# Graph attention, layer 2: the weighted sums of two beats issued as a pair, ahead of a later beat's scores

## Chip, cores and metric

One core of a Trainium2 chip runs the whole kernel. The metric is device time in microseconds (us). Before the change it is 3083.47 us, the median of three runs (3078.59 to 3084.39). The execution that the profile shows took 3076.43 us, and its instructions span 3074.7 us.

## What is computed

Eight graphs of 2048 nodes with 128 features pass through four attention layers that share one adjacency matrix. Each layer normalises x, applies a ReLU, and adds its attention to x. Layers 0, 1 and 3 are additive graph attention. Layer 2, which the change concerns, is dot-product attention with four heads of 32 features and no weights:

```
x = input_tensor.reshape(B, S, H, F // H)
scores = jnp.einsum('bihk,bjhk->bhij', x, x)
scores = leaky_relu(scores); masked where adj == 0
probs = jax.nn.softmax(scores, axis=-1)
out = jnp.einsum('bhij,bjhk->bihk', probs, x)
```

## The kernel before

**Two kinds of work are interleaved by hand.** Layers 0, 1 and 3 are cut into *tokens*. A token is one block of 128 source nodes against one half of the target nodes. Its `front` (line 396) is one VectorE operation that builds a 128x1024 tile `zg`. Its `back` (line 406) is eight matmuls of 129 columns, which add into PSUM banks 1 to 3. There are three `zg` buffers.

Layer 2 is cut into *beats*: 64 to an image (four heads by 16 source blocks), 512 in all. Beat q has three steps:

- `scores` (line 497): four TensorE matmuls of 512 columns into two pairs of PSUM banks, each pair followed by one ScalarE exponential (line 500) that writes half of a 128x2048 tile `z`. There are three `z` buffers. The bank pairs 4-5 and 6-7 are used in turn, and other steps (transposes, projections) use them too.
- `mask` (line 506): one VectorE operation that multiplies `z` by the adjacency and sums it.
- `weigh` (line 514): the sums. Four TensorE matmuls, each with 32 columns of weights at its own quarter of the array (`tile_position=(0, c * HD)`) and 512 columns of `z`, add into PSUM bank 0. When `weigh` is done, that `z` buffer is free for the scores of beat q + 3.

**The driving loop** (lines 626 to 641 before) walks over the beats. In pass q it issues the scores of q + 2, the mask of q + 1, one token if it is due, the sums of q, and further tokens until as many have been issued as the image's span asks for. The planner fixes only how tokens are spread over beats: images 1 to 5 have about 96 real tokens to 64 beats, image 0 about 34, image 6 63 and image 7 18, counted between the first sums of one image and of the next. The small stages of neighbouring layers (statistics, normalising, transposes, projections) hang on particular tokens.

**The order on an engine is not the order of the text.** The framework that builds the program schedules instructions by its own estimate of when they can start, and fixes the order on each engine. So four matmuls of a `weigh` may stand together, or as one and three with other matmuls between them. An engine then works through its own list in that order and waits where an operand is missing.

Of the kernel before, what the change touches and what calls it, by code (L numbers as in the profile page):

```python
# [37 lines left out]
def adj_preln_d4(ctx: ExitStack, tc: tile.TileContext, x, adj, w0, a0, w1, a1, w3, a3,  # L38
# [186 lines left out]
    def fast(ctx):  # L225
# [26 lines left out]
        def passed(us):  # L252
            for w in list(waiting):
                w[0] -= us
                if w[0] <= 0:
                    waiting.remove(w)
                    w[1]()
# [342 lines left out]
        def token():  # L600
            t = tokens[done[0]]
            if t:
                fronts(done[1] + 2)
                t[0].back(t[1])
                done[1] += 1
            for piece in pieces.get(done[0], ()):
                piece[0](*piece[1:])
            done[0] += 1
            passed(TOKEN_US)

        def beat(what, q):
            if q < B * 64:
                getattr(heads[q // 64], what)(q % 64)
# [12 lines left out]
        for q in range(B * 64):  # L626
            k, s = divmod(q, 64)
            t0, t1 = spans[k]
            until = t0 + (t1 - t0) * (s + 1) / 64
            beat("scores", q + 2)  # L630
            beat("mask", q + 1)
            if done[0] < until - 0.5:
                token()
            beat("weigh", q)
            passed(BEAT_US)
            if q % NB == 3 and q // NB + 1 < B * HEADS:
                g = q // NB + 1
                heads[g // HEADS].load(g % HEADS)
            while done[0] < until - 0.5:
                token()  # L640
# [173 lines left out]
    with tc.If(ok > 0) as arm:  # L814
        with ExitStack() as inner:
            fast(inner)
# [27 lines left out]
```

## Time and profile before

| What | Value |
|---|---|
| Time, median of 3 | 3083.47 us |
| TensorE (PE) busy | 2874.4 us, 93% |
| VectorE (DVE) busy | 2549.0 us, 83% |
| ScalarE (ACT) busy | 1808.8 us, 59% |
| Layer 2's beats run | from 383.7 us (first scores) to 2942 us (last sums) |
| Mean granted TensorE clock | 0.973 |
| DMA | 137.90 MB, mean 45 GB/s |

The span has three parts: the adjacency and the first tokens alone (to 384 us), the beats with tokens among them (to 2942 us), and the last tokens alone. The matmuls are float32. Each of those on lines 406 and 514 stands in the profile as two records, so "x8" on line 514 is one whole `weigh`, and "x16" on line 406 is one token. The ends of matmul records are modelled; what one costs is better read from the start of one group to the start of the next.

### The profile page before, as it was taken

To read this page: it belongs to the slowest core of one execution; us is meant where nothing else is said; L and a number is where in the kernel's file an instruction comes from. 1 tells how busy PE (TensorE), PEld (TensorE's weight loads), DVE (VectorE), ACT (ScalarE), POOL (GpSimd) and SP (SyncE) were. 2 spreads that over 40 slices of the span, in tenths; PEclk is the share of its full clock that TensorE was granted. 3 is DMA by queue.
4 is the path that set the end of the run, shared out by engine and by line. 5 is a ranking of instruction groups with operands and counts; after the bars stand their busy time and mean duration, and the time that the engine had idled before them with its cause. 6 is when DMAs were issued, how large, how long until landed. Compare 5 with 4: busy or idle time off the path is not lost.

```text
span 3074.7 us, 50065 instructions
## 1 busy us (share of the span) xinstructions
PE 2874.4 (93%) x20412; PEld 2112.7 (69%) x20415; DVE 2549.0 (83%) x3765; ACT 1808.8 (59%) x3113; POOL 168.2 (5%) x54
## 2 busy tenths in 40 slices
PE   3699989999999999999999999999999999988977
PEld 2699936677776776777677776777767766633657
DVE  5477769888898988988798997989879889987867
ACT  2343276758566558655676556665576666678652
POOL 1000000000010010000100001000000000000000
PEclk8699999999999999999999999999999999999998
DMA  6200411211113102121111212111021111312000
GB/s 223 55 1 1 97 41 45 56 32 32 32 35 69 49 17 67 32 59 25 49 44 27 52 32 66 32 39 45 15 73 32 42 28 39 79 38 55 8 8 22
DMA packets 141999, 137.90 MB, mean 45 GB/s; under 512 B 81728, under 2 KB 115136, under 8 KB 135616
## 3 DMA queue, kind: packets, MB, share of 16 engines
q1 hardware_dynamic: 134656, 125.87, 16.4%
q0 software_dynamic: 1152, 8.39, 0.7%
q8 instruction: 162, 2.65, 0.4%
q10 hardware_dynamic: 5952, 0.35, 0.2%
q14 instruction: 77, 0.63, 0.1%
HBM read 101.01 MB, written 33.55 MB: 44 GB/s over the span
## 4 chain that ended last, share of the span: by engine, by line
PE 72%; DVE 11%; ACT 8%; POOL 4%; issue 3%; DMA 2%; ACTq 0%; SPq 0%; POOLq 0%; DVEq 0%
PE ps L406 37%; PE ps L514 15%; PE ps L497 14%; DVE z L506 4%; DVE zg L396 4%; ACT z L500 3%; POOL rstdx L189 3%; PE ps L335 3%; ACT h L298 2%; PE ps L308 2%; PE ps L390 1%; DMA raw<-in_adj_dram 1%; DVE st L195 1%; POOL rstdh L189 1%; ACT wh L374 1%
## 5 line engine op out<-in xcount | busy, mean ns | idle before, releaser
L406 PEld LDWEIGHTS ps<-y,zg 128*128 128x128 f32 x12288 | 1499.2, 193 | 277.6 <-issue 132.5
L406 PE MATMUL ps<-y,zg 128*128 128x129 f32 x12288 | 1559.8, 279 | 18.3 <-DVE zg L396 14.8
L500 ACT ACTIVATE z<-ps,shift 128x1024 f32<-128x1024 f32 x1024 | 1098.7, 1117 | 679.7 <-PE ps L497 640.2
L506 DVE SCALAR_TENSOR_TENSOR z<-z,edge 128x2048 f32<-128x2048 f32 x512 | 1168.2, 2285 | 153.1 <-ACT z L500 151.2
L396 DVE SCALAR_TENSOR_TENSOR zg<-r,cr,edge 128x1024 f32<-128x1024 f32 x768 | 973.6, 1278 | 153.9 <-PE ps L406 125.6
L497 PE MATMUL ps<-m,s 128*128 128x512 f32 x2048 | 702.3, 438 | 59.9 <-ACT z L500 32.6
L514 PE MATMUL ps<-z,v 128*32 128x512 f32 x4096 | 645.9, 607 | 12.2 <-DVE z L506 12.2
L497 PEld LDWEIGHTS ps<-m,s 128*128 128x128 f32 x2048 | 339.1, 191 | 385.0 <-ACT z L500 152.3
L298 ACT ACTIVATE h<-x,nmrx,rstdx 128x128 f32<-128x128 f32 x512 | 216.2, 490 | 143.0 <-DVE nmrx L191 127.4
L189 POOL TENSOR_TENSOR rstdx<-varx,neg_half 128x16 f32<-128x16 f32 x32 | 123.4, 3859 | 2348.3 <-DVE varx L187 2069.9
L514 PEld LDWEIGHTS ps<-z,v 128*32 128x32 f32 x4096 | 93.5, 108 | 135.4 <-issue 63.4
L195 DVE BATCH_NORM_STATS2 st<-x 128x6 f32<-128x128 f32 x512 | 126.4, 268 | 7.9 <-DMA x<-in_x_dram 7.9
L335 PE MATMUL ps<-rhs,h_t 128*128 128x130 f32 x768 | 111.9, 290 | 3.2 <-ACT z L500 2.3
L335 PEld LDWEIGHTS ps<-rhs,h_t 128*128 128x128 f32 x768 | 100.1, 201 | 15.8 <-ACT z L500 11.8
L308 PE MATMUL ps<-ident,h 128*128 128x128 f32 x512 | 85.8, 284 | 24.1 <-ACT h L298 17.5
L325 ACT COPY h_t<-ps 128x512 f32<-128x512 f32 x96 | 56.1, 584 | 83.2 <-PE ps L308 83.0
L308 PEld LDWEIGHTS ps<-ident,h 128*128 128x128 f32 x512 | 61.5, 145 | 45.7 <-issue 19.3
L196 DVE BATCH_NORM_AGGREGATE mv<-st 128x2 f32<-128x6 f32 x512 | 82.1, 168 | 0.2
L191 DVE SCALAR_TENSOR_TENSOR nmrx<-mv,rstdx 128x16 f32<-128x16 f32 x32 | 5.6, 176 | 90.2 <-POOL rstdx L189 90.2
L429 ACT ACTIVATE oe<-ps,rs 128x128 f32<-128x128 f32 x128 | 53.5, 418 | 43.8 <-DVE rs L422 43.8
L351 ACT ACTIVATE y<-ps,y 128x128 f32<-128x128 f32 x256 | 73.2, 370 | 0.0
L391 ACT COPY r<-ps 128x1024 f32<-128x1024 f32 x48 | 48.4, 1011 | 41.0 <-PE ps L390 40.8
(95 smaller groups left out, 1061.9 us busy)
## 6 DMA issues: line engine op xcount, KB each, us to landing
s<-halves SPq DMA_DIRECT2D x256, 128.0 KB, 2.7
m<-halves SPq DMA_DIRECT2D x64, 512.0 KB, 5.5
raw<-in_adj_dram SPq DMA_DIRECT2D x8, 1024.0 KB, 7.3
raw<-in_adj_dram POOLq DMA_DIRECT2D x8, 1024.0 KB, 9.3
values<-h SPq DMA_DIRECT2D x32, 256.0 KB, 2.3
halves<-hi SPq DMA_DIRECT2D x128, 64.0 KB, 1.7
halves<-lo SPq DMA_DIRECT2D x128, 64.0 KB, 1.7
v<-values SPq DMA_DIRECT2D x32, 256.0 KB, 3.4
```

The lines of the kernel that those rows point to most:

```text
L189: nc.gpsimd.tensor_tensor(out=rstd, in0=var, in1=neg_half, op=OP.pow)
L195: nc.vector.bn_stats(out=st[:, n, :], in_=rows)
L196: nc.vector.bn_aggr(out=mv[:, n, :], in_=st[:, n, :])
L298: nc.scalar.activation(h, self.x[:, n, :], AF.Relu, scale=self.rstd[:, n:n + 1], bias=self.nmr[:, n:n + 1])
L308: nc.tensor.transpose(pk[:, k, :], self.h[q][:, k, :], ident)
L335: nc.tensor.matmul(pv[:, k, :C + 2], lhsT=self.h_t[q][:, k * P:(k + 1) * P], rhs=rhs, start=True, stop=True)
L396: nc.vector.scalar_tensor_tensor(z, self.r[half], self.cr[:, 0, jb:jb + 1], edge[:, jb, half * HN:(half + 1) * HN], op0=OP.max, op1=OP.mult)
L406: nc.tensor.matmul(ps[:, self.sums[half][i // 3], k * CE:(k + 1) * CE], lhsT=z[:, i * P:(i + 1) * P], rhs=self.y[:, jb, :], start=(jb == 0 ...
L497: nc.tensor.matmul(ps[:, lo + c, :], lhsT=self.S[h, jb // HB][:, at:at + P], rhs=self.M[h][:, (c2 * 2 + c) * 512:(c2 * 2 + c + 1) * 512], ...
L500: nc.scalar.activation(z[:, c2 * HN:(c2 + 1) * HN], ps[:, lo:lo + 2, :].rearrange("p b t -> p (b t)"), AF.Exp, bias=shift)
L506: nc.vector.scalar_tensor_tensor(self.z[s], self.z[s], 1.0, edge[:, jb, :], op0=OP.mult, op1=OP.mult, accum_out=self.den[:, h, jb:jb + 1])
L514: nc.tensor.matmul(ps[c * HD:(c + 1) * HD, 0, :], lhsT=self.V[h][:, jb, :], rhs=z[:, c * 512:(c + 1) * 512], start=jb == 0, stop=jb == NB - 1,
```

## The change

The sums leave the end of the pass. In each odd pass, the sums of the even beat before it and of its own beat are issued one after the other, at the head of the pass, in front of the scores of q + 2. In even passes none are issued. The purpose is to let the eight column-quarter matmuls of two beats stand next to each other on TensorE. The number and shape of the instructions stay the same, and so do the buffers.

```diff
             until = t0 + (t1 - t0) * (s + 1) / 64
+
+            if q % 2:
+                beat("weigh", q - 1)
+                beat("weigh", q)
             beat("scores", q + 2)
             beat("mask", q + 1)
             if done[0] < until - 0.5:
                 token()
-            beat("weigh", q)
             passed(BEAT_US)
```

## The prediction

> **What bounds the kernel now.** I read the busy shares first, then the chain that ended last, the groups of instructions, the stages, and last the timeline of TensorE alone.
>
> ```profile
> PE 2874.4 (93%) x20412; PEld 2112.7 (69%) x20415; DVE 2549.0 (83%) x3765; ACT 1808.8 (59%) x3113; POOL 168.2 (5%) x54
> PE 72%; DVE 11%; ACT 8%; POOL 4%; issue 3%; DMA 2%; ACTq 0%; SPq 0%; POOLq 0%; DVEq 0%
> PE ps L406 37%; PE ps L514 15%; PE ps L497 14%; DVE z L506 4%; DVE zg L396 4%; ACT z L500 3%; POOL rstdx L189 3%; PE ps L335 3%; ACT h L298 2%; PE ps L308 2%; PE ps L390 1%; DMA raw<-in_adj_dram 1%; DVE st L195 1%; POOL rstdh L189 1%; ACT wh L374 1%
> ```
>
> TensorE is busy 93% of the span and carries 72% of the chain; the sums (L514) alone are 15% of it. The groups give the prices:
>
> ```profile
> L406 PE MATMUL ps<-y,zg 128*128 128x129 f32 x12288 | 1559.8, 279 | 18.3 <-DVE zg L396 14.8
> L500 ACT ACTIVATE z<-ps,shift 128x1024 f32<-128x1024 f32 x1024 | 1098.7, 1117 | 679.7 <-PE ps L497 640.2
> L506 DVE SCALAR_TENSOR_TENSOR z<-z,edge 128x2048 f32<-128x2048 f32 x512 | 1168.2, 2285 | 153.1 <-ACT z L500 151.2
> L396 DVE SCALAR_TENSOR_TENSOR zg<-r,cr,edge 128x1024 f32<-128x1024 f32 x768 | 973.6, 1278 | 153.9 <-PE ps L406 125.6
> L497 PE MATMUL ps<-m,s 128*128 128x512 f32 x2048 | 702.3, 438 | 59.9 <-ACT z L500 32.6
> L514 PE MATMUL ps<-z,v 128*32 128x512 f32 x4096 | 645.9, 607 | 12.2 <-DVE z L506 12.2
> ```
>
> The idle columns matter. ACT waits for PE (640.2 us), DVE for PE and ACT, while PE's sums wait for the mask only 12.2 us in all, and its scores for the exponential (to free a bank pair) 32.6 us. PE sets the pace. The stages (span, then PE, PEld, DVE, ACT busy) show where that is less true; they are image 0, image 3 and image 7 of layer 2:
>
> ```profile
> 384.00:644.00 260.00, 249.74 (x1482) 140.69 (x1484) 208.75 (x233) 186.54 (x277) 5.76 (x2) 0.99 0.20 49
> 1355.00:1714.00 359.00, 348.96 (x2533) 259.84 (x2536) 312.56 (x464) 222.67 (x386) 19.98 (x5) 1.00 0.17 42
> 2719.00:2943.00 224.00, 200.96 (x1124) 99.72 (x1116) 185.30 (x239) 166.38 (x219) 9.65 (x2) 0.97 0.12 28
> ```
>
> In image 3 PE lacks 10 of 359 us, and DVE still has 46 us to spare. In image 7, with few tokens, PE lacks 23 of 224. Now PE's timeline (start, duration, group):
>
> ```profile
> 1016.08 1.05 PE L514 MATMUL ps<-z,v 128*32 128x512 f32 x2
> 1017.06 2.05 PE L406 MATMUL ps<-y,zg 128*128 128x129 f32 x16
> 1019.04 1.06 PE L514 MATMUL ps<-z,v 128*32 128x512 f32 x6
> 1020.03 1.20 PE L497 MATMUL ps<-m,s 128*128 128x512 f32 x4
> 1021.07 1.95 PE L406 MATMUL ps<-y,zg 128*128 128x129 f32 x16
> 1022.94 1.07 PE L514 MATMUL ps<-z,v 128*32 128x512 f32 x8
> ```
>
> One `weigh` is split here: a quarter alone takes 1017.06 - 1016.08 = 0.98 us, the other three 0.99 us. A whole one (x8) takes the same, 0.996 us in the median of 326 of them, start to start. So time is paid by the run, not by the matmul. And another place shows what a second set costs in the same run:
>
> ```profile
> 751.06 1.90 PE L514 MATMUL ps<-z,v 128*32 128x512 f32 x10
> 752.89 1.19 PE L497 MATMUL ps<-m,s 128*128 128x512 f32 x4
> ```
>
> Ten records are a whole set and one quarter more: 1.83 us, so the second set added 1.83 - 0.98 = 0.85 us.
>
> **What the Trainium skill says.** "TensorEngine Tiling (Array Packing)", Tiling Modes, says that a change of tiling mode (not merely of tile) drains the engine. The trace agrees with a cost at the borders: within a run, token records start 0.112 us apart, so 16 should take 1.79 us; the token between two sums above takes 1019.04 - 1017.06 = 1.98 us, 0.19 us more for one way out and one way in. "TensorE: Matmul & The Clock Gate", Part 3, says that column tiles run at once, some 4 ns apart; here the quarters start 7 ns apart. The same page, Part 2, says that matmuls stay in program order and only weight loads are pulled ahead, so a waiting sum holds everything queued behind it on PE.
>
> **The change, part by part.** Nothing is added or removed in kind: 2048 matmuls on L514, 2048 on L497 and 6144 on L406 in both. What differs is the built order on each engine, which I counted.
>
> *Sums on PE.* Before, the 2048 matmuls stand in 600 runs: 410 of four, and 84 of one and 86 of three from split beats. Counting one set for each time a quarter of the array comes round again, they make 607 sets. After, there are 457 runs, 113 of them of eight, and 579 sets. A run costs 0.98 + 0.19 = 1.17 us, a further set in it 0.86 us (two passes of 0.43 us, the middle of the readings). Before: 600 x 1.17 + 7 x 0.86 = 708 us. After: 457 x 1.17 + 122 x 0.86 = 640 us. The saving is 68 us. By image, from the same count and prices: 14 in image 0, 9 in each of images 1 to 4, 11 in image 5, 7 in image 6, and only 2 in image 7, where the order hardly changes. All lies on the engine that sets the end.
>
> *Scores on PE.* 795 runs become 750. A split costs nothing: one to four matmuls take 0.32, 0.57, 0.79 and 1.03 us, 0.24 each and about 0.08 a run, and the token before starts them 0.08 us early (0.030 instead of 0.112 us after its last record). Zero. The other matmuls, ACT, DVE and DMA keep their counts and durations: zero, under PE's work.
>
> *The wait for the mask.* A pair now needs the mask of its second beat. Behind a waiting sum on PE stand the scores of q + 2 and the tokens; ACT waits for those scores, and DVE for ACT. From the last score matmul to a ready `z` at least 1.12 (exponential) + 2.29 + 0.08 (mask and its read-out) + about 0.1 = 3.6 us pass, and up to 1.28 more if a token's `zg` is ahead on DVE: 4.9 us. I summed the PE work, at the prices above, between each beat's last score and its first sum in the built order. In images 1 to 6 the mean is 8.9 to 11.5 us before and 8.6 to 10.6 after: two beats of slack, hence no wait. Under 5 us are 43 beats before and 56 after, nearly all in images 0 and 7. There PE idles 10.3 + 22.9 = 33 us before, with 42 such beats: 0.79 us each. Thirteen more: +10 us. The bounds are 0 (idle in those images has other causes too) and 13 x 2.4 = 31 us (a whole mask each).
>
> *The wait for a bank pair.* Without sums between them, the scores of two beats come closer: after a pair, "scores, one token, scores" is 1.9 us apart, then a long stretch follows. A pair of banks is free 1.12 us plus a hop after its matmuls, if ACT isn't in other work (each normalising row holds it 0.49 us). Reuse within 2.5 us of PE work happens 210 times before and 311 after. The 32.6 us of before are 0.155 us each: 101 x 0.155 = +15 us (bounds 0 and 30).
>
> *Tokens in twos.* The after order has 86 runs of exactly two tokens, before 20, with the same three `zg` buffers. All gaps before L406 in the beats' part are 13 us before; I allow +8 (bounds 0 and 20). In image 3 DVE goes from 312.6 / 359 = 87% to 312.6 / 350 = 89%, so it doesn't become the bound.
>
> Sum: -68 + 10 + 15 + 8 = -35 us, 3083.5 - 35 = 3048 us.
>
> **Rivals.** *A, the forecast*, 3048 us. *B, the waits eat the gain*: uneven spacing makes ACT and DVE work in bursts and PE idle for them. With every wait at its upper bound, 31 + 30 + 20 = 81 us, nothing is left; at about four fifths, 65 us, it ends at 3080. For it: DVE is at 87% and ACT sits in the loop PE, ACT, DVE, PE of image 7. Against: the mean slack of 8.6 us and more. *C, slower*: pairing makes PE stand at every run of eight until the second mask is done. If 113 runs wait 0.75 us (somewhat over half a `zg`), 85 us are added: 3083.5 - 68 + 85 = 3100. For it: the text puts the mask of q only one pass ahead of its sum, where it used to be more. Against: the built order, which keeps two beats between scores and sums. *D, the whole gain* with no more than a few us of new waits: 3020 us; for it, the 12.2 us of mask waits in the whole span.
>
> **How the numbers follow.** A 0.55, B 0.25, C 0.13, D 0.07. A and D are faster by over 0.2% (6.2 us); of B I give 0.10 to faster, 0.08 to no difference and 0.07 to slower; C is slower. Faster 0.72, same 0.08, slower 0.20. The range runs from 3022, which takes in half of D, to 3090, which takes in B and leaves out C. What is left out is about 0.04 + 0.13, with a little of A's and B's edges.
>
> **What would show it.** L514 should have about 457 runs, with x16 groups whose starts lie 1.83 us from the next group's; the total of those runs start to start falls by some 40 us, and the rest shows in tokens of 1.81 to 1.88 us where they were 1.98. DVE's and ACT's busy times stay at 2549 and 1809. The idle before L514 for the mask should stay under some 25 us, that before L497 for the exponential under some 50. Image 3 should take about 353 us, image 0 about 250, image 7 224 to 230. It is wrong if a second set in a run costs 0.98 us after all (then 122 x 0.12 = 15 us less), if sums wait for the mask in the images with many tokens, or if the idle before L497 doubles.

## The result and the profile after

The changed kernel takes 3039.82 us (median; 3036.10 to 3041.98), the kernel before, timed beside it on the same chip, 3083.93 us. The ratio is 0.9857, with a 95% interval of 0.9839 to 0.9876: 44 us less (38 to 50). The prediction was 3048 us.

The profiled spans are 3036.1 and 3074.7 us, a difference of 38.6 us. It lies in the beats (2559.2 to 2526.4 us, -32.8) and ahead of them (383.7 to 376.2 us, -7.5, in code that the change doesn't touch). The tail after the beats takes 133.5 us where it took 131.8. The other 5 us of the 44 aren't in the profiles: the execution profiled of the kernel before was 7 us under its median, that of the changed one 2 us under. The images in us, from first sums to first sums (image 0 from its first scores, image 7 to the last sums):

| Image | 0 | 1 | 2 | 3 | 4 | 5 | 6 | 7 |
|---|---|---|---|---|---|---|---|---|
| before | 260 | 352 | 359 | 359 | 362 | 362 | 281 | 224 |
| after | 251 | 347 | 356 | 356 | 357 | 354 | 279 | 226 |

First the busy shares and the chain that ended last, of the kernel after:

```profile
PE 2816.8 (93%) x20415; PEld 2116.3 (70%) x20415; DVE 2544.2 (84%) x3765; ACT 1804.7 (59%) x3113; POOL 165.3 (5%) x54
PE 67%; DVE 15%; ACT 9%; POOL 4%; issue 3%; DMA 1%; ACTq 0%; POOLq 0%; SPq 0%; DVEq 0%
```

TensorE's share of the chain fell from 72% to 67%, VectorE's rose from 11% to 15%. DVE's and ACT's busy times didn't move. So more of the end now hangs on other engines, although TensorE has less to do. The groups say where (line, engine, operation, then busy us and mean ns, then the idle time before it and what ended it):

```profile
L406 PE MATMUL ps<-y,zg 128*128 128x129 f32 x12288 | 1526.9, 278 | 22.0 <-DVE zg L396 16.1
L500 ACT ACTIVATE z<-ps,shift 128x1024 f32<-128x1024 f32 x1024 | 1093.5, 1117 | 683.7 <-PE ps L497 636.0
L506 DVE SCALAR_TENSOR_TENSOR z<-z,edge 128x2048 f32<-128x2048 f32 x512 | 1166.6, 2282 | 147.6 <-ACT z L500 146.2
L497 PE MATMUL ps<-m,s 128*128 128x512 f32 x2048 | 689.5, 435 | 58.1 <-ACT z L500 26.6
L514 PE MATMUL ps<-z,v 128*32 128x512 f32 x4096 | 600.8, 607 | 28.3 <-DVE z L506 27.9
```

The sums lost 45 us of modelled busy time. Their wait for the mask went from 12.2 to 27.9 us. The scores' wait for the exponential fell, from 32.6 to 26.6 us. The stages of images 0, 3 and 7 (span, then PE, PEld, DVE, ACT busy):

```profile
376.00:627.00 251.00, 239.37 (x1497) 142.64 (x1496) 209.22 (x235) 184.10 (x276) 5.76 (x2) 0.98 0.23 52
1331.00:1686.00 355.00, 341.83 (x2526) 260.95 (x2519) 311.19 (x464) 222.53 (x385) 19.98 (x5) 1.00 0.17 42
2677.00:2903.00 226.00, 200.06 (x1123) 100.53 (x1121) 186.19 (x240) 166.71 (x219) 9.66 (x2) 0.96 0.13 27
```

In image 3 PE now lacks 13 of 355 us, where it lacked 10 of 359. And TensorE's timeline, in image 3, shows the pairs themselves (start, duration, group):

```profile
1598.73 3.74 PE L406 MATMUL ps<-y,zg 128*128 128x129 f32 x32
1602.39 1.92 PE L514 MATMUL ps<-z,v 128*32 128x512 f32 x16
1604.25 1.20 PE L497 MATMUL ps<-m,s 128*128 128x512 f32 x4
1605.28 1.95 PE L406 MATMUL ps<-y,zg 128*128 128x129 f32 x16
1606.98 1.17 PE L497 MATMUL ps<-m,s 128*128 128x512 f32 x4
```

A pair takes 1604.25 - 1602.39 = 1.86 us from its start to the next group's. The token after the scores takes 1606.98 - 1605.28 = 1.70 us, since it has no sum on either side. Over the whole trace a run of 8 records takes 996 ns in the median, one of 16 takes 1854 ns (113 of them). A token takes 1.98 us between two sums, 1.81 after sums and before scores, 1.88 the other way round, 1.70 between two scores. Added up start to start, the sums fell from 639.4 us in 600 runs to 597.8 us in 457, by 41.6 us.

The beats' time on TensorE can be cut into work (start to next start, less the idle that the trace shows) and that idle:

| us in the beats | before | after | difference |
|---|---|---|---|
| sums, without idle | 606.4 | 570.7 | -35.7 |
| tokens, without idle | 1103.2 | 1086.4 | -16.8 |
| scores, without idle | 594.9 | 588.2 | -6.7 |
| other matmuls, without idle | 169.5 | 174.7 | +5.2 |
| idle that the trace shows | 85.2 | 106.4 | +21.2 |

The work fell by 54 us, and 21 us came back as idle: for the mask +15.7, for the exponential -6.2 ahead of scores and +3 ahead of other matmuls, for ScalarE's small steps (rows and copies, lines 298, 301, 325, 346, 391, 430 and 432) about +10, for `zg` 0 (7.5 us in both).

One thing doesn't show as idle: TensorE's granted clock. The trace has it over time, and in the beats it is either 1.0 or 0.5. One place where it is 0.5, in the changed kernel (a stretch as above, with the clock after the busy times, then TensorE's timeline):

```profile
1129.00:1135.70 6.70, 5.39 (x24) 5.29 (x25) 3.73 (x5) 4.35 (x9) 0.00 (x0) 0.50 0.37 98
1130.31 0.80 PE L497 MATMUL ps<-m,s 128*128 128x512 f32 x1 [2.85 <-DVE lo L470]
1130.90 6.94 PE L406 MATMUL ps<-y,zg 128*128 128x129 f32 x40
```

The 40 records of tokens take 6.87 us to the next group (at 1137.77 us), where 40 x 0.112 = 4.48 us would do. Over the whole of the beats, records of tokens start 112 ns apart (median) at a clock of 1.0 and 214 ns at 0.5. So such a stretch costs about half of the time in it in which TensorE works. Before, 58 us of the beats are at 0.5 (49 of them work), after, 65 us (50 work): by this estimate 24 and 25 us are lost, which doesn't change the account. Between experiments the loss differs more, and is given below where it matters. In the changed kernel each of the eleven such stretches has 1.3 us or more of TensorE's idle time in the 7 us before it; that waits bring the clock down is likely, but no run varied one of the two alone.

### The profile page after: what moved, and what is told of

Read it like the earlier page. It is cut to its first block, busy times and chain, and to the rows that moved or that the text cites. A ratio compares the mean times of both kernels' runs of the same rounds, so it can differ in the third digit from the quotient of the medians.

```text
span 3036.1 us, 50090 instructions
## 1 busy us (share of the span) xinstructions
PE 2816.8 (93%) x20415; PEld 2116.3 (70%) x20415; DVE 2544.2 (84%) x3765; ACT 1804.7 (59%) x3113; POOL 165.3 (5%) x54
## 4 chain that ended last, share of the span: by engine, by line
PE 67%; DVE 15%; ACT 9%; POOL 4%; issue 3%; DMA 1%; ACTq 0%; POOLq 0%; SPq 0%; DVEq 0%
PE ps L406 34%; PE ps L514 14%; PE ps L497 13%; DVE z L506 6%; DVE zg L396 5%; POOL rstdx L189 3%; ACT z L500 3%; PE ps L335 3%; ACT h L298 2%; PE ps L390 1%; PE ps L308 1%; DVE st L195 1%; POOL rstdh L189 1%; DMA raw<-in_adj_dram 1%; ACT wh L374 1%
## 5 line engine op out<-in xcount | busy, mean ns | idle before, releaser
L406 PE MATMUL ps<-y,zg 128*128 128x129 f32 x12288 | 1526.9, 278 | 22.0 <-DVE zg L396 16.1
L497 PE MATMUL ps<-m,s 128*128 128x512 f32 x2048 | 689.5, 435 | 58.1 <-ACT z L500 26.6
L514 PE MATMUL ps<-z,v 128*32 128x512 f32 x4096 | 600.8, 607 | 28.3 <-DVE z L506 27.9
L298 ACT ACTIVATE h<-x,nmrx,rstdx 128x128 f32<-128x128 f32 x512 | 216.8, 490 | 128.9 <-DVE nmrx L191 123.3
L189 POOL TENSOR_TENSOR rstdx<-varx,neg_half 128x16 f32<-128x16 f32 x32 | 121.6, 3801 | 2317.8 <-DVE varx L187 2097.1
L514 PEld LDWEIGHTS ps<-z,v 128*32 128x32 f32 x4096 | 102.0, 108 | 200.1 <-issue 101.1
L308 PEld LDWEIGHTS ps<-ident,h 128*128 128x128 f32 x512 | 60.9, 144 | 52.5 <-issue 20.9
L325 ACT COPY h_t<-ps 128x512 f32<-128x512 f32 x96 | 56.1, 584 | 59.2 <-PE ps L308 59.2
L390 PE MATMUL ps<-ident,cr 128*128 128x128 f32 x384 | 53.9, 287 | 16.0 <-ACT r L391 11.0
```

Source lines behind the costliest of these rows:

```text
L189: nc.gpsimd.tensor_tensor(out=rstd, in0=var, in1=neg_half, op=OP.pow)
L298: nc.scalar.activation(h, self.x[:, n, :], AF.Relu, scale=self.rstd[:, n:n + 1], bias=self.nmr[:, n:n + 1])
L308: nc.tensor.transpose(pk[:, k, :], self.h[q][:, k, :], ident)
L390: nc.tensor.transpose(pk[:, k, :], self.cr[:, 1, n:n + 1].to_broadcast([P, P]), ident)
L406: nc.tensor.matmul(ps[:, self.sums[half][i // 3], k * CE:(k + 1) * CE], lhsT=z[:, i * P:(i + 1) * P], rhs=self.y[:, jb, :], start=(jb == 0 ...
L497: nc.tensor.matmul(ps[:, lo + c, :], lhsT=self.S[h, jb // HB][:, at:at + P], rhs=self.M[h][:, (c2 * 2 + c) * 512:(c2 * 2 + c + 1) * 512], ...
```

## The experiments

Two theories stood at the start. The first: TensorE pays by the run and by the set, so a kernel with fewer runs and sets is faster by that much, less small waits. The second: it is the place of the sums or their pairing as such that counts, or TensorE isn't the bound and the saved work turns into waits. The ratios are to the kernel before, beside which each was timed; runs and sets are counted in the built order, as in the prediction.

### The pair at the end of the pass, and single sums at its head

The change has two parts: sums in pairs, and sums in front of the scores. The pairing alone (e1):

```diff
             if done[0] < until - 0.5:
                 token()
-            beat("weigh", q)
+            if q % 2:
+                beat("weigh", q - 1)
+                beat("weigh", q)
             passed(BEAT_US)
```

> The sums of two beats are issued as a pair, but where they stood before: at the end of the odd pass, behind the scores and a token. Theory 1 (TensorE pays 1.17 us for each run of sums and 0.86 us for each further set in it): the built order has 485 runs and 664 sets, against 600 and 607 before and 457 and 579 after, so the sums cost 721 us against 708 and 640; the time is 3085 to 3105 us, no gain. Theory 2 (pairing as such pays): 113 or so pairs are kept, 3040 to 3055 us.

Measured: 3119.77 us, ratio 1.0125 (1.0107 to 1.0144), slower than either end of what the first theory gave. Pairs there are: 115 runs of eight, as many as in the changed kernel (113). But 235 runs are of one or three matmuls, where 170 were before, so there are 485 runs and 664 sets, more than the 607 of before, and the sums take 704.5 us start to start. That pairs as such pay, the second theory of this run, is thereby out. One row of the groups of this kernel tells what else happened:

```profile
L500 ACT ACTIVATE z<-ps,shift 128x1024 f32<-128x1024 f32 x1024 | 1092.1, 1117 | 805.2 <-PE ps L514 584.5 <-PE ps L497 218.7
```

The exponential now mostly waits for the sums (584.5 us; 35.9 before). With three `z` buffers, the scores of q + 2 can't be exponentiated until the sums of q - 1 are done, and these come last in the pass. So an order in the text that pairs the sums is not enough: behind the scores, it ties the `z` buffers up. (By the counts, 13 of the 41 us above the kernel before are dearer sums. Visible idle in the beats is 104 us instead of 85, and the clock estimate gives a loss of 34 us instead of 24. That the buffers bring this idle is argued from the row, not tested.)

The place alone (e2):

```diff
+            beat("weigh", q)
             beat("scores", q + 2)
             beat("mask", q + 1)
             if done[0] < until - 0.5:
                 token()
-            beat("weigh", q)
```

> The sums of each beat stand at the head of their own pass, in front of the scores, not paired. Theory 1: 575 runs and 576 sets, 674 us, 34 us less work than before; but 82 beats instead of 43 have under 5 us of TensorE work between their last score and their sums, at up to 0.79 us each, so 10 to 34 us is given back: 3050 to 3085 us. Theory 2 (the place ahead of the scores is what pays): 3040 us as in the changed kernel.

Measured: 3074.13 us, ratio 0.9989 (0.9979 to 0.9999). There are 575 runs and 576 sets. By the prediction's prices that is 575 x 1.17 + 0.86 = 674 us, 34 less than before; 3 to 5 us came. The work on TensorE in the beats did fall by 34 us, but 30 us came back as idle: the sums' wait for the mask rose to 24.5 us and the scores' wait for the exponential to 41.8. The place alone gives next to nothing, and the pairs where the sums stood before lose: neither half of the change has its gain.

### Whole sums without pairs

The kernel before, with the four matmuls of a `weigh` kept together by a higher priority in the scheduler (e3):

```diff
                 for c in range(4):
-                    nc.tensor.matmul(ps[c * HD:(c + 1) * HD, 0, :], lhsT=self.V[h][:, jb, :],
+                  with tc.high_priority():
+                    nc.tensor.matmul(ps[c * HD:(c + 1) * HD, 0, :], lhsT=self.V[h][:, jb, :],
```

> The kernel before, with the sums' instructions at the highest priority in the scheduler, so that no set is split: 507 runs, 512 sets, no pairs to speak of. Theory 1: the sums cost 598 us, 110 us less than before and 42 us less than after, and the groups on line 514 sum to about 500 us start to start. But they come soon after their masks: 194 beats have under 5 us of slack instead of 43. If each costs 0.79 us, 119 us come back and the time is about 3090 us; if only the real excess counts, 3000 to 3050 us. The idle before the sums for the mask must be well over 28 us. Theory 2 (splits cost little, waits decide): slower than before, over 3100 us.

Measured: 3045.33 us, ratio 0.9888 (0.9872 to 0.9905), with 507 runs and 512 sets; the sums take 535.1 us. So hardly any pair is needed for three quarters of the change's gain: whole sums do it. Priced, it should have given 507 x 1.17 + 5 x 0.86 - 708 = -110 us; a third came. The sums' row in the groups shows one taker of the rest:

```profile
L515 PE MATMUL ps<-z,v 128*32 128x512 f32 x4096 | 555.4, 615 | 51.3 <-DVE z L506 50.4
```

The visible idle of TensorE in the beats is 132 us here, 47 more than before. And its clock is at 0.5 in 99 us of the beats, where it was in 58: by the estimate above a loss of 41 us instead of 24.

### All sums in pairs

The sums of an even beat are made to depend on the mask of the odd one, so that the scheduler can't separate them, with a priority that keeps all eight matmuls together (e4):

```diff
+                  with tc.high_priority(offset=100):
+                    mm = nc.tensor.matmul(ps[c * HD:(c + 1) * HD, 0, :], lhsT=self.V[h][:, jb, :],
...
+                    if s % 2 == 0:
+                        tc.add_manual_dep(mm.ins, self.mk[s + 1].ins.name, mybir.DependencyInfo(
+                            mybir.DependencyClass.Sync, mybir.DependencyReason.DATA), reason="pair")
```

> The changed kernel, with the first sums of a pair made to wait for the mask of its second beat, and the sums ahead of other work in the scheduler: all 512 sets stand in 256 runs of eight. Theory 1: the sums cost 520 us, 188 us less than before and 120 less than after; the slack is as before (45 beats under 5 us), bank pairs are reused within 2.5 us 362 times instead of 210 (+24 us): 2925 to 2975 us, unless VectorE (2545 us busy) becomes the bound. Theory 2 (the pair's wait for the second mask costs about as much as it saves): no faster than the changed kernel, 3040 us or more, with over 100 us of idle before the sums.

Measured: 3033.95 us, ratio 0.9853 (0.9836 to 0.9870), the same as the change within the intervals. There are 256 runs, each of two sets, and the sums take 505.1 us, 93 less than in the changed kernel. None of it reached the end: visible idle in the beats is 170 us instead of 106, and 113 us of the beats are at a clock of 0.5 instead of 65, by the estimate above a loss of 47 us instead of 25. From the view of line 500 in this kernel, what ended ScalarE's idle time ahead of the exponentials (us, times):

```profile
  PE ps L497: 381.3, 197
  PE ps L515: 219.2, 96
```

and the sums' row of the groups:

```profile
L515 PE MATMUL ps<-z,v 128*32 128x512 f32 x4096 | 511.7, 619 | 63.5 <-DVE z L506 62.5
```

The loop is closed: sums wait for the second mask (62.5 us), and exponentials wait for those sums to free `z` (219.2 us, 96 times). The chain gives TensorE 54%, where it had 67%. The first theory, that work saved on TensorE is time saved, falls here.

The same without the priority, which is e4's edit less its `with` line, and so with fewer whole pairs (e10):

> The first sums of a pair wait for the mask of its second beat, as in the run with all sums paired, but the sums have no priority over other work in the scheduler: 293 runs and 540 sets, 555 us against 520 there and 640 in the changed kernel; the mean slack of images 2 to 5 is 11.0 us against 9.3 there and 10.6. Theory 1 (what the all-paired kernel lost, it lost to slack): about 35 us more work than there, but waits nearer to those of the changed kernel: 2990 to 3025 us. Theory 2 (fewer runs always bring more waits, whatever the slack): 3030 us or more.

Measured: 3032.50 us, ratio 0.9853 (0.9830 to 0.9876); 293 runs, 540 sets, mask wait 43.6 us, exponentials waiting for sums about 240 us. The time lies in the range of its second theory. Without the priority it is the same, so the priority isn't what held e4 back.

### More room for `z`, and half a mask

A fourth `z` buffer for the paired kernel, paid for with smaller pools elsewhere (`s` 3 to 2, `hi` and `lo` 2 to 1) (e6):

```diff
-                z = self.z[s] = big.tile([P, N], F32, tag="z", name="z", bufs=3)
+                z = self.z[s] = big.tile([P, N], F32, tag="z", name="z", bufs=4)
```

> All sums in 256 runs of eight as before, with a fourth buffer for z; the room comes from one buffer less for s, hi and lo. Theory 1 (in the kernel with all sums paired, the three z buffers are the bound: exponentials wait 219 us for the sums to free a buffer): that wait falls under 80 us and the time to 2950 to 3000 us. Theory 2 (the latency from scores over exponential and mask to the sums is the bound, whatever the buffers): idle before the sums stays at 60 us and the time is 3020 us or more.

Measured: 3022.07 us, ratio 0.9818 (0.9797 to 0.9840), 12 us less than e4. The same view of line 500:

```profile
  PE ps L497: 543.0, 294
  PE ps L515: 34.1, 22
```

The wait for the sums went from 219.2 to 34.1 us, and yet only 12 us came of it: the scores' wait for the exponential rose to 56.1 us, from 33.3. The buffers were a wait, not the bound. The time is in the range of the second theory, though the idle before the sums fell from 63.5 to 46.4 us.

In e4, the mask over half the columns of `z` (e7):

```diff
-                self.mk[s] = nc.vector.scalar_tensor_tensor(self.z[s], self.z[s], 1.0, edge[:, jb, :],
+                self.mk[s] = nc.vector.scalar_tensor_tensor(self.z[s][:, :HN], self.z[s][:, :HN], 1.0, edge[:, jb, :HN],
```

> All sums in 256 runs of eight, three z buffers, and the mask over the first 1024 columns only (the second half of each z stays unmasked), so that a mask takes about 1.2 us instead of 2.37. Theory 1 (the 188 us that the runs save are real, and VectorE's mask hides them): with it short, TensorE is the bound again, 2890 to 2960 us. Theory 2 (the borders and splits never cost what I priced): the time stays over 3000 us.

Measured: 2971.88 us, ratio 0.9653 (0.9631 to 0.9674), 62 us less than e4, between the two theories and nearer the first. The mask takes 1.22 us instead of 2.28. So VectorE is part of what holds e4 back (about 9 of the 62 us are the clock by the estimate above, at 0.5 in 82 us of the beats instead of 113; and the data here are others), but 125 us of visible idle in the beats remain even with half a mask.

With four `z` buffers, pairs bound without priority, and the scores one beat further ahead (e11):

```diff
-            beat("scores", q + 2)
+            beat("scores", q + 3)
```

> Pairs bound as in the run before, a fourth z buffer (one buffer less for s, hi and lo), and the scores issued one beat earlier: 334 runs and 578 sets, 601 us, 39 us less than in the changed kernel; the mean slack rises from 10.6 to 15.5 us in images 2 to 5, and only 11 beats have under 5 us of slack. Theory 1 (slack decides what the pairs give): idle before the sums under 10 us, and 2970 to 3010 us. Theory 2 (the two bank pairs and ScalarE, not the slack, bound the rest): idle before the scores stays at 50 us or more, and the time is 3020 us or more.

Measured: 3015.60 us, ratio 0.9792 (0.9768 to 0.9816), between its two theories and faster than both kernels: its interval lies below that of the change (0.9839 to 0.9876). 334 runs and 578 sets, hardly fewer sets than the change has (579), but

```profile
L514 PE MATMUL ps<-z,v 128*32 128x512 f32 x4096 | 572.0, 606 | 11.1 <-DVE z L506 10.3 <-ACT o_t L522 0.4
```

the wait for the mask is 10.3 us, against 43.6 in e10. e6 has the same buffers, spends 65 us less on its sums (493.4 us; 558.6 here) and is no faster: room for the mask is worth as much as those further sets.

### Is TensorE the bound? The sums twice

In the changed kernel each beat's four matmuls of the sums are issued twice (e8); the scheduler lays the program out by its own rules again:

```diff
-                for c in range(4):
+                for i in range(8):
+                    c = i % 4
```

> The changed kernel, with each beat's four sum matmuls issued twice in a row, so the layer 2 sums are doubled. The built order has 367 runs and 1077 sets: 367 x 1.17 + 710 x 0.86 = 1040 us against 640. Theory 1 (TensorE is the bound all along, a further set in a run costs 0.86 us): 400 us more, less some 30 us of waits that the longer runs fill: 3400 to 3440 us. Theory 2 (a further set costs as much as a run of its own, 0.98 to 1.17 us): 3500 us and more.

Measured: 3318.04 us, ratio 1.0777 (1.0753 to 1.0801). From TensorE's timeline of this kernel:

```profile
1011.18 3.64 PE L515 MATMUL ps<-z,v 128*32 128x512 f32 x32
1014.75 1.19 PE L497 MATMUL ps<-m,s 128*128 128x512 f32 x4
```

A run of 32 records (four sets) takes 3.57 us, against 1.854 for two sets: (3571 - 1854) / 2 = 858 ns a set. That is the prediction's 0.86 us, and the second theory falls. With 367 runs and 1077 sets the added work is 367 x 1.17 + 710 x 0.86 - 640 = 400 us. The time rose by 278 us over the changed kernel, and so stayed under the first theory's range too. About 120 us of added TensorE work cost nothing. Visible idle in the beats fell from 106 to 34 us, which is 72 of the 120. The clock is at 0.5 in 7 us of the beats instead of 65, a loss of 2 us instead of 25 by the estimate above. The other 25 or so stay open. In the changed kernel, then, the beats' 2526 us have room for some 120 us more work on TensorE. It is the engine with the most to do, but not the only one that sets the end.

### Where the new mask waits come from

The prediction had no mask waits in images 1 to 6. Before, there are none: 6.9 us in image 0 and 5.3 in image 7. After, by image, 7.5, 1.5, 3.1, 3.1, 3.0, 3.1, 1.6 and 5.1 us: the whole growth lies in images 1 to 6. One of these places, from the timeline of all engines of the changed kernel (in brackets, idle time before and what ended it):

```profile
1615.23 3.78 POOL L189 TENSOR_TENSOR rstdx<-varx,neg_half 128x16 f32<-128x16 f32 x1 [77.09 <-DVE varx L187]
...
1619.05 0.17 DVE L191 SCALAR_TENSOR_TENSOR nmrx<-mv,rstdx 128x16 f32<-128x16 f32 x1 [2.79 <-POOL rstdx L189]
...
1619.13 1.06 PE L514 MATMUL ps<-z,v 128*32 128x512 f32 x8
1619.14 2.28 DVE L506 SCALAR_TENSOR_TENSOR z<-z,edge 128x2048 f32<-128x2048 f32 x1
...
1621.49 1.06 PE L514 MATMUL ps<-z,v 128*32 128x512 f32 x8 [1.29 <-DVE z L506]
```

GpSimd computes the inverse standard deviation with a power, in 3.78 us. VectorE stands 2.79 us at the product behind it (line 191), and the mask is queued after that product. It starts at 1619.14, and the second half of the pair waits 1.29 us for it. (The first half has gone ahead, because its own mask was done.) VectorE waits in this way at every one of the 40 groups of statistics, in both kernels: 90.2 + 22.5 us before, 90.0 + 22.4 after. The page of the kernel before has the first of these figures:

```profile
L191 DVE SCALAR_TENSOR_TENSOR nmrx<-mv,rstdx 128x16 f32<-128x16 f32 x32 | 5.6, 176 | 90.2 <-POOL rstdx L189 90.2
```

Three experiments take the wait away.

The product on GpSimd, so that VectorE doesn't wait for the power (e5):

```diff
+        nc.vector.tensor_scalar(nm, mv[:, :, 0], -1.0, None, op0=OP.mult)
-        nc.vector.scalar_tensor_tensor(nmr, mv[:, :, 0], -1.0, rstd, op0=OP.mult, op1=OP.mult)
+        nc.gpsimd.tensor_tensor(out=nmr, in0=nm, in1=rstd, op=OP.mult)
```

> The changed kernel, with the product -mean x rstd taken off VectorE: VectorE negates the mean before GpSimd's power, and GpSimd multiplies, so VectorE no longer stands still until GpSimd has finished. Theory 1 (the new waits of the sums in images 1 to 6, 1.3 to 1.6 us each, come from masks that stand on VectorE behind that product, which waits 2.8 us for GpSimd): those waits (15 us in all) go, the sums' order costs 631 us instead of 640, and the time is 3010 to 3030 us; VectorE's idle of 90 us for GpSimd goes. Theory 2 (the waits come from the pairing itself): the idle before the sums stays at 25 us or more and the time within 3030 to 3042 us.

Measured: 3056.04 us, ratio 0.9924 (0.9907 to 0.9942), 16 us slower than the change (21 by the ratios) and outside both theories. Its groups:

```profile
L516 PE MATMUL ps<-z,v 128*32 128x512 f32 x4096 | 599.2, 619 | 4.4 <-DVE z L508 3.9 <-ACT o_t L521 0.4
L499 PE MATMUL ps<-m,s 128*128 128x512 f32 x2048 | 698.9, 440 | 76.4 <-ACT z L502 61.7 <-ACT h_t L327 5.5 <-DVE lo L472 3.0
L300 ACT ACTIVATE h<-x,nmrx,rstdx 128x128 f32<-128x128 f32 x512 | 218.1, 489 | 164.0 <-POOL nmrx L193 160.8 <-PE ps L310 3.0
```

The mask wait is gone (3.9 us). But now ScalarE stands at the normalising rows (160.8 us for GpSimd; 123.3 for VectorE's product in the changed kernel), with exponentials queued behind, and the scores wait 61.7 us. The wait changed its engine. The scheduler also laid out the whole program anew, and 106 us of the beats are at a clock of 0.5 instead of 65 (a loss of 49 us instead of 25 by the estimate above), so that the causes can't be told apart in the time.

The power on VectorE (a bit-shift seed and three Newton steps, eleven small operations of about 0.17 us in place of one on GpSimd; e9):

```diff
-        nc.gpsimd.tensor_tensor(out=rstd, in0=var, in1=neg_half, op=OP.pow)
+        nc.vector.tensor_scalar(seed, var.bitcast(I32), 1, None, op0=OP.logical_shift_right)
+        nc.vector.tensor_scalar(rstd.bitcast(I32), seed, -1.0, 1597463007.0, op0=OP.mult, op1=OP.add)
...
+        for _ in range(3):
+            nc.vector.tensor_mul(t, var, rstd)
+            nc.vector.scalar_tensor_tensor(t, t, -0.5, rstd, op0=OP.mult, op1=OP.mult)
+            nc.vector.scalar_tensor_tensor(rstd, t, 1.5, rstd, op0=OP.add, op1=OP.mult)
```

> The changed kernel, with the power -0.5 of the variance computed on VectorE (a seed from the bits of the number and three Newton steps, 11 small operations) instead of by GpSimd in 3.8 us, so that neither VectorE nor ScalarE waits for GpSimd. The sums' order costs 648 us against 640 (469 runs, 584 sets). Theory 1 (the sums' new waits come from masks queued behind a wait for GpSimd; in the run with the product on GpSimd the wait only moved to ScalarE): the idle before the sums in images 1 to 6 goes, and the idle before the scores doesn't rise as it did there: 3005 to 3030 us. Theory 2 (GpSimd's latency is hidden, and more VectorE work costs): 3040 us or more.

Measured: 3080.49 us, ratio 1.0004 (0.9993 to 1.0015), far from what the theory of the GpSimd wait gave, and within what the second gave. The mask wait is 7.5 us. But the order differs again (469 runs, 584 sets), VectorE has 48 us more to do (2592), and there is new idle: 29.9 us of the scores for the additive attention's row operations (`r`), 16.4 us of other matmuls for the exponential. And 137 us of the beats are at a clock of 0.5 instead of 65, by the estimate above a loss of 48 us instead of 25. With the 8 us that the counts price and 14 us more of visible idle in the beats, this is about the whole of the 41 us between the two kernels. As a test of one wait it fails: too much else moved.

So the last one had to leave the order alone. In the changed kernel the power becomes a multiplication by -0.1 on the same engine and tiles (e12). The built order on every engine is that of the changed kernel:

```diff
-    nc.vector.memset(neg_half, -0.5)
+    nc.vector.memset(neg_half, -0.1)
...
-        nc.gpsimd.tensor_tensor(out=rstd, in0=var, in1=neg_half, op=OP.pow)
+        nc.gpsimd.tensor_tensor(out=rstd, in0=var, in1=neg_half, op=OP.mult)
```

> The changed kernel in exactly its own order on every engine; only GpSimd's power (3.8 us) is a multiplication (about 0.2 to 0.5 us), so the normalisation is left out in effect (each row is scaled by -0.1 x variance). Theory 1 (masks behind the product that waits for GpSimd cause the new waits of the sums; the two runs that took this wait away lost it again because their whole order changed): the idle before the sums in images 1 to 6 falls from 16 us to under 3, VectorE's 90 us of idle for GpSimd to under 10, and with the order kept the time falls by 15 to 50 us, a ratio to the kernel before of 0.969 to 0.981. Theory 2 (the wait is harmless, as hidden elsewhere): ratio 0.983 to 0.988, as for the changed kernel.

Measured: 2955.44 us, ratio 0.9593 (0.9572 to 0.9614): 84 us less than the change (81 by the ratios), more than the 15 to 50 forecast. Its busy shares and chain, and rows of its groups:

```profile
PE 2796.5 (95%) x20412; PEld 2107.8 (71%) x20415; DVE 2547.1 (86%) x3765; ACT 1802.2 (61%) x3113; POOL 58.2 (2%) x54
PE 84%; ACT 8%; DVE 4%; issue 2%; DMA 1%; ACTq 0%; POOL 0%; SPq 0%; POOLq 0%; DVEq 0%
L514 PE MATMUL ps<-z,v 128*32 128x512 f32 x4096 | 597.5, 605 | 5.2 <-DVE z L506 4.8 <-ACT o_t L519 0.4
L189 POOL TENSOR_TENSOR rstdx<-varx,neg_half 128x16 f32<-128x16 f32 x32 | 35.8, 1122 | 2343.8 <-DVE varx L187 2121.6 <-ACT z L500 190.4 <-DVE mv L196 31.9
```

and the place of the pair above in its timeline:

```profile
1571.50 1.10 POOL L189 TENSOR_TENSOR rstdx<-varx,neg_half 128x16 f32<-128x16 f32 x1 [78.08 <-DVE varx L187]
1572.64 0.18 DVE L191 SCALAR_TENSOR_TENSOR nmrx<-mv,rstdx 128x16 f32<-128x16 f32 x1
1572.73 2.28 DVE L506 SCALAR_TENSOR_TENSOR z<-z,edge 128x2048 f32<-128x2048 f32 x1
1575.40 1.93 PE L514 MATMUL ps<-z,v 128*32 128x512 f32 x16
```

The pair is whole, and TensorE doesn't wait in it. VectorE's idle time before line 191 is 2 us instead of 112. The mask waits of images 1 to 6 are 1.2 us in all instead of 15.3; those of images 0 and 7 are 3.6 instead of 12.6. TensorE's share of the chain is 84%. Since the order is the same, the cause of the new mask waits is shown: it is VectorE standing at the product behind GpSimd's power.

The 84 us are more than these waits. There are 52 us less visible idle in the beats (106 to 54) and 12 us less in the stretches ahead of and behind the beats (376.2 to 370.3, 133.5 to 127.5). And TensorE's clock is at 0.5 in 31 us of the beats instead of 65, by the estimate above a loss of 14 us instead of 25. Some 8 us stay open. (As means, 0.987 and 0.994 in the beats; rounded to two digits both read 0.99.) Whether the shorter waits or the other data raised the clock, this run doesn't separate; VectorE's and ScalarE's busy times are within 3 us of the changed kernel's. The wait behind the power is in the kernel before just as long, so the 84 us can't be taken for what the change lost. Of this wait the change brought 15 us onto its sums; what the quick operation would give in the kernel before wasn't run.

## Why the prediction was right, and where it was not

**The sums, -68 us.** Right in kind, somewhat too large: the work on TensorE fell by 54. The price of a set (0.98 us for the first, 0.86 for a further one) held in both kernels and in e8. In the prediction's terms, 143 fewer runs and 115 more further sets make -41 us for the sums without borders (start to start -41.6, without idle -35.7), and 143 borders of 0.19 us make -27 (the tokens and scores gave -23.5). The last 5 us are the other matmuls, +5.2, nearly all at the transposes of line 308 (47.6 to 52.5), which I had at zero. That a `weigh` need only stay whole, which e3 shows to be worth three quarters of the gain, I had in the count, but hadn't named.

**Scores' splits, nothing.** The scores' work fell by 6.7 us, which fits fewer borders next to sums. VectorE's and ScalarE's busy times are 2544 and 1805 us, as expected.

**The wait for the mask, +10 us.** This step failed, though its sum looks close: +15.7 us, 27.9 in all where I gave 25 as the limit. That sums wait for the mask in images with many tokens was one of my signs of being wrong, and it came. I put all of it into images 0 and 7, and said "two beats of slack, hence no wait" of images 1 to 6. Images 0 and 7 changed by +0.4 us together, and images 1 to 6 got 15.3. My reckoning of what can stand ahead of a mask on VectorE took in one `zg` (1.28 us), and left out an operation that waits: the product of line 191 holds the queue for 2.8 us. The page of the kernel before shows it, as idle of VectorE "<-POOL rstdx L189", and the chain had POOL at 4%, which I read past. An engine that is busy 5% holds up another at 40 places, each time for most of its operation.

**The bank pair, +15 us.** Wrong: that idle fell from 32.6 to 26.6 us, with more close reuses than before. A count of close reuses isn't a count of waits; to make one it would have needed the time at which ScalarE takes up the exponential. What of it the pairs' spacing did, no run separates.

**Tokens in twos, +8 us.** The wait of tokens for `zg` in the beats is 7.5 us in both. What I didn't list is about 10 us of idle for ScalarE's small steps and 3 for the exponential ahead of other matmuls. So the waits came to +21 us against my +33, with the parts wrong and the sum within its bounds.

**The total.** For the beats I had -35 us; the profile has -33. Two errors offset each other: 14 us too much saved, 12 us too much waited. That the total came so close is luck in part. The other 7.5 us of the profiled difference lie ahead of the beats, where I forecast nothing and where the change does nothing. With the 5 us between the profiled executions and the medians, that makes the measured -44 us larger than my -35. Why the stretch ahead is shorter stays open; in the profiles of e1 to e11 it takes between 377 and 385 us, so 7.5 us is about what it varies by.

**The images.** Image 0 was to take about 250 us and took 251, image 7 224 to 230 and took 226, image 3 353 and took 355 to 356: the missing 3 us are as much as its mask waits (3.1), which stand beside a forecast of none.

**Rivals.** B (waits eat the gain, 3080 us) and C (pairs stand at the second mask, 3100 us) didn't come to pass, but both mechanisms are there. e4 is B: it saves another 93 us on the sums and gains nothing. The place shown above is C: a run of eight that stands for its second mask; but the sums wait for a mask 21 times in all, where C had 113. That "PE sets the pace", with which the prediction began, is only a part: e8 hides 120 us of added work. "TensorE: Matmul & The Clock Gate" in the Trainium skill, Part 2, has matmuls stay in program order, and on this rests that a waiting sum holds up what stands behind it. e4's trace agrees:

```profile
1483.64 2.17 PE L406 MATMUL ps<-y,zg 128*128 128x129 f32 x18
1488.43 2.90 PE L515 MATMUL ps<-z,v 128*32 128x512 f32 x16 [2.62 <-DVE z L506]
```

The last 2 of the 18 records are the first of a new token. Its other 14 need the same `zg`, but they start at 1491.26 us, behind the sums, while TensorE stood 2.62 us for the mask.

**What stays open.** What the quick GpSimd operation would give in the kernel before, and in e4: not run. Whether e4's waits beyond `z` and half a mask are GpSimd's too. What brings TensorE's clock to 0.5 in stretches of the beats. And how to get the power off VectorE's path with the order kept: e5 and e9 take it off, but the scheduler's order changed with them, and they came out slower than the change.

## What to carry to other kernels

Count runs and sets of small-tile matmuls in the built order, and price both: keeping a set whole and next to another of its kind is worth a per-run cost, but only as long as the consumer's buffers and the producer's queue leave room for it. Before you call a wait impossible because there is slack, look in each engine's queue for an instruction that itself waits on a slow engine; it holds everything behind it, however idle that slow engine is on the whole. To test one wait, change a duration and leave the order alone; an edit that makes a scheduler lay out the program again tests everything at once. And compare the granted clock over time, in more than two digits: it can hold what the idle columns don't.

## What the runs showed of the hardware that was not expected

- GpSimd's power of a 128x16 float32 tile takes 3.78 us in the timeline above (mean 3.80 over 32, from 2.90 to 4.78), the multiplication of tiles of the same shape 1.12 us in the mean (0.22 to 2.11). The small VectorE operations on the same tiles take 0.17 to 0.18 us.
- A further set of four 32-column matmuls of 512 float32 columns costs 0.858 us (runs of two and of four sets agree), 0.996 us for the first. Going into and out of such runs costs about 0.19 us, seen in the matmuls around them (tokens of 1.98 us between sums, 1.79 by their own spacing). "TensorEngine Tiling (Array Packing)", Tiling Modes, in the Trainium skill says that a change of mode drains the engine; the trace agrees with a cost at each change, and this is its size here.
- TensorE's granted clock drops to 0.5 in stretches of 3.4 to 10.2 us among the beats, and token records then start 214 ns apart instead of 112. It does so for 7 us of the beats in e8, 31 in e12, 58 in the kernel before, 65 in the changed one, 113 in e4 and 137 in e9. None of this shows in the idle time before matmuls.
